# A two-layer convolution kernel: one program order for all engines in layer one, stores of a piece held back, borders written later

## The chip, the cores and the metric

The kernel runs on one core of a Trainium2 chip. The metric is the device time of one execution in microseconds, the median of several runs. A profiled execution of the same program gives the trace; it is one execution and has its own time.

## The reference, cut to what matters

The input x is 32 images of 8 channels, 256 x 256, float32. Layer zero runs on a group-normalised copy (4 groups of 2 channels each), layer one on the result of layer zero.

```python
def layer0(x):                      # x: group-normalised
    grid = x
    for _ in range(15):             # the lattice
        mapped = 3.9 * grid * (1 - grid)
        local = conv3x3(mapped, K_local, per channel)
        grid = 0.85 * (0.7 * mapped + 0.3 * local) + 0.15 * x
    cml = clip(grid, 1e-4, 1 - 1e-4)
    h = relu(conv3x3(x, Wp) + bp)                   # 8 -> 128 channels
    nca = sigmoid(conv1x1(h, Wu) + bu)              # 128 -> 8
    gin = concat([x, cml, nca])
    g = sigmoid(conv1x1(relu(conv3x3(gin, Wg1) + bg1), Wg2) + bg2)
    return g * cml + (1 - g) * nca

def layer1(x):                      # x: group-normalised
    sx, sw = 127 / max|x|, 127 / max|w|             # over the whole batch
    return conv3x3(round(x * sx), round(w * sw)) / (sx * sw) + bias

y = x + layer0(gn(x))
out = y + layer1(gn(y))
```

## The kernel before, in words

The program's "layer one" is its first big block (everything of `layer0` above); the second block, "layer two", does `layer1` and is not touched.

The images go in 8 groups of 4. For every group four kinds of work are needed, each written as a Python generator that emits some instructions and then yields a weight:

- **normalise** (L285 on, `prep`): for an image and a pair of channels ("piece"): load x (`xr`), statistics, mean and deviation over partitions by two tiny matmuls (L313, L324), scale in place (L331), then three copies: `xq` (ScalarE, L336, columns regrouped by four), `hi` (VectorE, L342, rounded) and `lo` (GpSimd, L343, the rest). Six DMAs store them to DRAM scratch (L345, L352). `xq`, `hi` and `lo` have one buffer each. A job is two pieces: channel pairs 0 and 1, or 2 and 3. A group has eight jobs.
- **lattice**: for each of the 8 channels, all four images of the group at once, 15 steps. A step is three tiles; a tile is 12 matmuls (L487) into two PSUM banks, and on VectorE two `gt` (L495) and two `m` (L500) operations; GpSimd mends an edge (L504). After tiles two and three SP issues the exchange of rows between neighbouring partitions (`m_a<-m_a`, L450 and L451). A channel of four images is a "unit"; its loads (`d_a`, `d_b`) and the stores of its result go into a list `later`, from which `background(3)` issues three DMAs after each tile (L444).
- **nca**: for each image, the hidden convolution (L567) in pairs of PSUM banks that ScalarE empties with relu (L577), then L584 down to 8 channels and a sigmoid. Rows are loaded to `im` (L537, L545).
- **gate**: for each image of the group before, ten pieces: loads `nb`, `cq`, `xb`; 54 matmuls in three parts (L759); r1 (L771); a small matmul (L725), sigmoid (L727); then GpSimd's `d` and `f` (L730, L732) and VectorE's product, sum, statistics, maximum and minimum (L734 to L745).

`together(lattice, filler)` emits a lattice step, then filler until both stand at the same share of their nominal weights; `both` mixes nca, gate and normalisation of the next group in the same way. So every lattice step on TensorE is followed by some filler on TensorE. Lattice tiles, the hidden convolution and the small matmuls share six PSUM banks (tag `pt`).

What sets the order: on TensorE the order in which the program emits (`manual_schedule` for PE). On VectorE, ScalarE, GpSimd and SP's DMA queue a planner puts the instructions in order before the run, by its own model of times and with the program's order as priority; on the chip each engine then runs its list in order. `reuse_waits` is not given for the pools of layer one.

Ahead of it all stands a preparation: constants, and zeros written to the border rows of 68 DRAM scratch tensors (4 DMAs each, ACT's queue, L199 and L202) from a tile `zt` in a pool that is freed before layer one's pools are opened. Normalisation of channel pairs 0 and 1 of the first four images is emitted before the lattice starts, pairs 2 and 3 as the first filler.

Of the kernel before, what the change touches and what calls it, by code (L numbers as in the profile page):

```python
# [31 lines left out]
F32 = mybir.dt.float32  # L32
# [8 lines left out]
P = 128  # L41
C = 8
# [71 lines left out]
def kernel(  # L114
# [46 lines left out]
    rstd_y = cp.tile([P, B], F32, name="rstd_y")  # L161
    dev_y = cp.tile([P, B], F32, name="dev_y")


# [7 lines left out]
    with tc.tile_pool(name="prep", bufs=1) as pp, tc.tile_pool(name="prep2", bufs=2) as pp2:  # L172
# [20 lines left out]

        zt = pp.tile([P, PW], F32, name="zt")
        G.memset(zt, 0.0)
        for t, n, w in (
            *((t, 2 * C, PW) for t in xp_s), *((t, C, W) for t in (*cm_s, *nc_s, *y_s))
        ):
            nc.scalar.dma_start(dram_ap(t, 0, [[w, n], [1, w]]), zt[:n, :w])  # L199
            for i in range(0, 11, 5):  # L200
                m = min(5, 11 - i) * n
                nc.scalar.dma_start(dram_ap(t, (257 + i) * n * w, [[w, m], [1, w]]), zt[:m, :w])  # L202

# [53 lines left out]
    with ExitStack() as one:  # L257

        one.enter_context(tc.manual_schedule(engines={mybir.EngineType.PE}))
        pool = lambda name, bufs, **kw: one.enter_context(tc.tile_pool(name=name, bufs=bufs, **kw))  # L260
        xp, sp2, gp, bp2, st = pool("xp", 4), pool("sp2", 1), pool("gp", 3), pool("bp2", 2), pool("st", 2)
        imp, hp, wk, wk1, np_ = pool("imp", 3), pool("hp", 12), pool("wk", 2), pool("wk1", 1), pool("np", 1)
        ps_c, ps_a = pool("ps_c", 6, space=PSUM), pool("ps_a", 2, space=PSUM)
# [24 lines left out]
        def normalise(jobs):  # L288

            def begin(b, half):
                xrs = []
                mv = st.tile([P, 2, 2], F32, name="mv", tag="mv")
                stats = st.tile([P, 2, 2, 6], F32, name="stats", tag="stats")
                for i in range(2):
                    g = 2 * half + i
                    xr = xp.tile([P, 2, 2, W], F32, name="xr", tag="xr")
                    nc.sync.dma_start(  # L300
                        xr.rearrange("p c h w -> p (c h) w"),
                        dram_ap(x, (b * C + 2 * g) * H * W, [[W, P], [P * W, 4], [1, W]]),
                    )
                    for j in range(2):
                        V.bn_stats(stats[:, i, j, :], xr[:, j].rearrange("p h w -> p (h w)"))
                    V.bn_aggr(mv[:, i, :], stats[:, i].rearrange("p j s -> p (j s)"))
                    xrs.append(xr)
                return b, half, xrs, mv

            def scale(b, half, xrs, mv):  # L310
                gs = slice(2 * half, 2 * half + 2)
                pm = ps_c.tile([P, 512], F32, name="pm", tag="pt")
                T.matmul(pm[:, 0:2], avg, mv[:, :, 0], start=True, stop=True)  # L313
                m, rstd = mean_x[:, b, gs], rstd_x[:, b, gs]
                V.tensor_copy(m, pm[:, 0:2])
                e = st.tile([P, 2], F32, name="e", tag="e")
                V.tensor_tensor(e, mv[:, :, 0], m, ALU.subtract)
                V.tensor_tensor(e, e, e, ALU.mult)
                V.tensor_tensor(e, e, mv[:, :, 1], ALU.add)
                return e  # L320

            def end(b, half, xrs, e):
                pv = ps_c.tile([P, 512], F32, name="pv", tag="pt")
                T.matmul(pv[:, 0:2], avg, e, start=True, stop=True)  # L324
                rstd = rstd_x[:, b, 2 * half : 2 * half + 2]
                V.tensor_scalar(rstd, pv[:, 0:2], GN_EPS, None, ALU.add)
                G.tensor_tensor(rstd, rstd, mhalf[:, 0:2], ALU.pow)
                for i, xr in enumerate(xrs):
                    g = 2 * half + i
                    flat = xr.rearrange("p c h w -> p (c h w)")  # L330
                    V.tensor_scalar(  # L331
                        flat, flat, mean_x[:, b, g : g + 1], rstd_x[:, b, g : g + 1],
                        ALU.subtract, ALU.mult,
                    )
                    xq = sp2.tile([P, 2, 2, 4, NJ], F32, name="xq", tag="xq")
                    S.activation(  # L336
                        xq.rearrange("p c h q j -> p (c h) q j"),
                        xr.rearrange("p c h (j q) -> p (c h) q j", q=4),
                        AF.Copy,
                    )  # L340
                    inner = lambda t: t[:, :, :, 1 : 1 + W]
                    V.tensor_copy(inner(hi), xr)  # L342
                    G.tensor_tensor(inner(lo), xr, inner(hi).bitcast(F32), ALU.subtract)  # L343
                    for h in range(2):
                        nc.sync.dma_start(  # L345
                            dram_ap(
                                xq_s[b % NBUF], (2 * g * H + P * h) * W, [[W, P], [H * W, 2], [1, W]]
                            ),
                            xq[:, :, h].rearrange("p c q j -> p c (q j)"),
                        )  # L350
                        for j, src in enumerate((hi, lo)):
                            nc.sync.dma_start(  # L352
                                dram_ap(
                                    xp_s[b % NBUF],
                                    (1 + P * h) * ROW + (C * j + 2 * g) * PW,
                                    [[ROW, P], [PW, 2], [1, PW]],
                                ),
                                src.bitcast(F32)[:, :, h, :],
                            )
                    yield 1.0  # L360
                ready.add((b, half))

            ahead = None
            for job in [*jobs, None]:
                now = begin(*job) if job else None
                yield 1.0
                if ahead:
                    e = scale(*ahead)
                    yield 1.0
                    yield from end(*ahead[:3], e)  # L370
                ahead = now

# [3 lines left out]
        def lattice(g):  # L376


            def load(u):


                c, out, dmas = u % C, [], []
                assert all((u // C * GB + i, c // 4) in ready for i in range(GB))
                for s in range(2):
# [57 lines left out]
            def background(n):  # L442
                for _ in range(min(n, len(later))):
                    nc.sync.dma_start(*later.pop(0))  # L444
                    issued[0] += 1

            def exchange(t, k):
# [109 lines left out]
        def nca(b):  # L557
# [80 lines left out]
            im = ahead  # L638
            if (b + 1, 0) in ready and (b + 1, 1) in ready:
                loaded[b + 1] = rows(b + 1, 0, 0)  # L640
# [26 lines left out]
        def stage(b, p, sc):  # L667
# [11 lines left out]
            )  # L679
            for k in range(n):  # L680
                G.tensor_copy(  # L681
                    cmb[:, k, 1 : 1 + W].rearrange("p (j q) -> p j q", q=4),
                    cq[:, k, :].rearrange("p (q j) -> p j q", q=4),
                )
            xb = bp2.tile([P, 2, W], F32, name="xb", tag="xb", bufs=3)
            if p in (0, 9):
                G.memset(xb, 0.0)
            for k in range(n):
# [6 lines left out]
                        [[W, r1_ - r0], [H * W, C], [1, W]],  # L695
                    ),
                )
            for k in range(n):
# [13 lines left out]
        def gate(b):  # L712
# [35 lines left out]
            last = done = None  # L748
            sc, ahead = staged.pop(b, None) or begin_gate(b)
            for p in range(10):  # L750
# [5 lines left out]
                for s, t in ((0, xnb), (1, cmb), (2, nb)):  # L756
# [11 lines left out]
                    if s < 2:  # L768
                        yield 2.6
                r1 = wk.tile([P, 512], F32, name="r1", tag="r1")  # L770
                S.activation(r1[:, : n * W], pa[:, : n * W], AF.Relu, bias=bv[:, 0:1])  # L771
# [93 lines left out]

        def prep(g, halves):
            return normalise([(b, half) for half in halves for b in range(g * GB, g * GB + GB)])

# [11 lines left out]
        T_NCA, T_GATE, T_PREP, T_LATTICE = 520.0, 340.0, 34.0, 8 * 45 * 1.97  # L880
        for _ in prep(0, (0,)):
            pass
        for g in range(NG):
            fill, t = images(nca, g), T_NCA
            if g:
                fill, t = both(fill, t, after(g - 1, images(gate, g - 1)), T_GATE), t + T_GATE
            if g + 1 < NG:
                fill, t = both(fill, t, prep(g + 1, (0, 1)), T_PREP), t + T_PREP
            if g == 0:
                fill, t = chain(prep(0, (1,)), fill), t + 20.0  # L890
            together(lattice(g), T_LATTICE, fill, t)
        for _ in images(gate, NG - 1):
            pass
# [115 lines left out]
```

## Time and profile before

| what | value |
|---|---|
| median of 3 runs | 14360.28 us (14354.44 to 14362.28) |
| profiled execution, time | 14416.5 us |
| its span, first to last instruction | 14414.7 us |
| mean granted TensorE clock | 0.963 |
| busy: TensorE matmul, VectorE, ScalarE, GpSimd | 92%, 57%, 28%, 17% of the span |
| first lattice matmuls | 201 us, in a steady row from 220 us |
| first matmul of the hidden convolution | 305 us, in a steady row from 316 us |
| layer two | from about 13640 us |

The span runs from the first to the last instruction. Busy shares are means over stages; a stage is read from its own stretch of time. A wait is written "engine line waiting <- engine line waited for"; "SPq" is SP's DMA queue. The granted clock of TensorE is either 1.0 or 0.5 at any time, and a matmul takes twice as long at 0.5.

### The profile page before, as it was taken

Reading aid. Unit: us, or ns where it says so; the run is one execution under the profiler, and the core shown is the slowest. Engines: PE = TensorE matmul, PEld = TensorE weight load, DVE = VectorE, ACT = ScalarE, POOL = GpSimd, SP = SyncE. Lnnn points to the kernel's source line nnn. Section 1 sums busy time; section 2 is a strip of 40 time slices with the busy share of each in tenths; the row PEclk is TensorE's granted clock in tenths of the full one; section 3 lists DMA queues with packets and bytes.
Section 4 is the critical chain, followed back from the end, with each engine's and each line's share of the span. In section 5 each row is a group of like instructions: output and inputs, shape, how many; then the busy total and the mean of one; then the engine's idle time right before and its main releaser. Section 6 shows DMA issues by size and latency. Waiting matters only on the chain.

```text
span 14414.7 us, 229163 instructions
## 1 busy us (share of the span) xinstructions
PE 13267.4 (92%) x81728; PEld 6423.3 (45%) x81728; DVE 8213.1 (57%) x16290; ACT 4039.8 (28%) x6274; POOL 2445.9 (17%) x4266
## 2 busy tenths in 40 slices
PE   2999999999999999999999999999999999999833
PEld 1554444444444444444444444444444444444311
DVE  3555555555555555555555555555555555555576
ACT  1333232232222222222322223222323222222122
POOL 1111111111111111111111111111111111112300
PEclk9999999999999999999999999999999999999966
DMA  5444444444444444444444434444444433333465
GB/s 148 93 97 92 90 103 106 103 94 100 110 94 100 99 106 94 103 100 95 100 103 107 98 93 106 110 94 94 104 104 98 103 88 88 80 83 78 122 195 176
DMA packets 2259559, 1496.74 MB, mean 104 GB/s; under 512 B 1061248, under 2 KB 2229504, under 8 KB 2258304
## 3 DMA queue, kind: packets, MB, share of 16 engines
q1 hardware_dynamic: 2176976, 1401.95, 41.9%
q10 hardware_dynamic: 81456, 80.12, 1.7%
q8 instruction: 664, 10.88, 0.3%
q14 instruction: 463, 3.79, 0.1%
HBM read 866.48 MB, written 478.69 MB: 93 GB/s over the span
## 4 chain that ended last, share of the span: by engine, by line
PE 70%; DMA 9%; DVE 9%; SPq 5%; issue 3%; POOL 2%; ACT 1%; ACTq 1%; POOLq 0%; DVEq 0%
PE pt L487 31%; PE ph L567 18%; PE pa L759 13%; PE acc L584 7%; DVE gt L495 2%; DMA im<-xp_s 1%; PE pg L725 1%; DMA xp_s<-lo 1%; SPq L545 1%; DVE m_b L500 1%; DMA xb<-in_x_dram 1%; DMA m_a<-m_a 1%; DMA out_dram<-ob 1%; SPq L960 1%; PE pt L953 1%
## 5 line engine op out<-in xcount | busy, mean ns | idle before, releaser
L487 PE MATMUL pt<-m_a,lw 128*64 128x390 f32 x17280 | 5827.0, 497 | 186.4 <-DMA m_a<-m_a 122.4
L487 PE MATMUL pt<-m_b,lw 128*64 128x384 f32 x17280 | 5796.6, 492 | 19.2 <-DVE m_b L410 18.0
L577 ACT ACTIVATE h<-ph,bp_sb 128x512 f32<-128x512 f32 x4096 | 2584.6, 684 | 6491.5 <-PE ph L567 6423.0
L487 PEld LDWEIGHTS pt<-m_a,lw 128*64 128x64 f32 x17280 | 2298.4, 138 | 1884.0 <-issue 1681.2
L487 PEld LDWEIGHTS pt<-m_b,lw 128*64 128x64 f32 x17280 | 2306.6, 138 | 1560.0 <-issue 1423.6
L567 PE MATMUL ph<-im,wp_hi 48*128 48x512 f32 x12288 | 2800.2, 419 | 174.2 <-DVE gt L495 113.1
L567 PE MATMUL ph<-im,wp_lo 48*128 48x512 f32 x12288 | 2675.2, 402 | 0.0
L495 DVE SCALAR_TENSOR_TENSOR gt<-pt,d_b 128x390 f32<-128x390 f32 x2880 | 1605.3, 557 | 1714.7 <-PE pt L487 1711.2
L495 DVE SCALAR_TENSOR_TENSOR gt<-pt,d_a 128x384 f32<-128x384 f32 x2880 | 1580.3, 549 | 1694.5 <-PE pt L487 1694.1
L504 POOL TENSOR_TENSOR m_b<-m_b,junk 128x12 f32<-128x12 f32 x2688 | 795.5, 296 | 8193.8 <-DVE m_b L500 7517.2
L567 PEld LDWEIGHTS ph<-im,wp_hi 48*128 48x128 f32 x12288 | 1417.5, 189 | 1081.7 <-DVE gt L495 303.9
L500 DVE SCALAR_TENSOR_TENSOR m_b<-gt 128x390 f32<-128x390 f32 x2688 | 1546.1, 575 | 44.5 <-DVE gt L495 2.3
L500 DVE SCALAR_TENSOR_TENSOR m_a<-gt 128x384 f32<-128x384 f32 x2688 | 1522.3, 566 | 17.2
L567 PEld LDWEIGHTS ph<-im,wp_lo 48*128 48x128 f32 x12288 | 1417.0, 189 | 217.3
L584 PE MATMUL acc<-h,wu_z 128*32 128x512 f32 x8320 | 1165.6, 603 | 6.1 <-ACT nca L602 5.5
L759 PE MATMUL pa<-xnb,gw 128*64 128x512 f32 (+1 forms) x3840 | 879.9, 588 | 43.7 <-DVE xnb L700 43.5
L759 PE MATMUL pa<-cmb,gw 128*64 128x512 f32 (+1 forms) x3840 | 857.6, 577 | 17.4 <-POOL cmb L681 17.4
L759 PE MATMUL pa<-nb,gw 128*64 128x512 f32 (+1 forms) x3840 | 863.6, 576 | 0.0
L730 POOL TENSOR_TENSOR d<-cmb,nb 128x512 f32<-128x512 f32 x320 | 502.9, 1572 | 1460.6 <-DVE gate L734 1028.5
L700 DVE TENSOR_SCALAR xnb<-xb,sc 128x256 f32<-128x256 f32 x608 | 290.7, 493 | 796.7 <-DMA xb<-in_x_dram 759.5
L953 PE MATMUL pt<-qt,qw 128*128 128x512 bf16 (+1 forms) x960 | 269.5, 451 | 477.0 <-ACT ob L954 425.4
L734 DVE TENSOR_TENSOR gate<-gate,d 128x512 f32<-128x512 f32 x320 | 217.4, 679 | 764.7 <-ACT gate L727 756.7
(132 smaller groups left out, 6928.0 us busy)
## 6 DMA issues: line engine op xcount, KB each, us to landing
im<-xp_s SPq DMA_DIRECT2D x1152, 193.5 KB
im<-xp_s SPq DMA_DIRECT2D x1216, 96.8 KB
d_a<-xq_s SPq DMA_DIRECT2D x2048, 36.0 KB
nb<-nc_s SPq DMA_DIRECT2D x288, 256.0 KB
cq<-cm_s SPq DMA_DIRECT2D x288, 256.0 KB
yb<-y_s ACTq DMA_DIRECT2D x29, 2432.0 KB
xb<-in_x_dram SPq DMA_DIRECT2D x544, 128.0 KB
xp_s<-hi SPq DMA_DIRECT2D x256, 258.0 KB
```

The costliest lines, as they stand in the source:

```text
L487: T.matmul(pt[half], lw[:, c, k, half], beside if part == 2 else own, start=part < 2, stop=part > 0,)
L495: V.scalar_tensor_tensor(gt, pt, FLOOR, d[:, ts, :], ALU.max, ALU.add)
L500: V.scalar_tensor_tensor(to, gt, 1.0, gt, ALU.subtract, ALU.mult)
L504: G.tensor_tensor(edge, edge, junk.unsqueeze(1).to_broadcast([P, 6, 2]), ALU.mult)
L567: T.matmul(ph[:, :n].rearrange("p (h w) -> p h w", w=W), w[64 * i : 64 * i + 48, dx, :], rhs[:, :, dx : dx + W], start=(dx == 0 and w is w ...
L577: S.activation(h[:, :n], ph[:, :n], AF.Relu, bias=bp_sb)
L584: T.matmul(acc[32 * g : 32 * g + 32, :cols], wu_z[:, 24 - 8 * i : 56 - 8 * i], h, start=first, stop=last,)
L700: V.tensor_scalar(xnb[:, k, 1 : 1 + W], xb[:, k, :], sc[:, i : i + 1], sc[:, 1:2], ALU.subtract, ALU.mult,)
L730: G.tensor_tensor(three(d), cmb[:, :n, 1 : 1 + W], nin, ALU.subtract)
L734: V.tensor_tensor(y[:, :cols], gt[:, :cols], d[:, :cols], ALU.mult)
L759: T.matmul(three[half], gw[:, s * 3 + dx, half], t[:, :n, dx : dx + W], start=(i == 0), stop=(i == 8),)
L953: T.matmul(pt, qw[:, dx, :], q[:, k0 : k0 + n, dx : dx + W], start=(dx == 0), stop=(dx == 2))
```

## The change

1. All engines and SP's queue keep the order in which the program emits in layer one (`manual_schedule()` without a list of engines), and the pools wait tile by tile for memory that others have used.
2. The zeros lie in a constant tile of 64 columns. Each border DMA reads it several times over (256-byte or 172-byte pieces). Sixteen border DMAs, those of the first four `xp_s`, stay in front; 256 are issued from SP's queue by `background` during the first group, in the places that `later` leaves.
3. Normalisation: loads are split from statistics (`take`), which come after the work on the job before. The six stores of a piece are not issued after it but just before the next piece is scaled (`pending`).
4. First group: pair 0 of the four images before the lattice, then pair 1, then jobs of pairs 2 and 3, as the first filler.
5. Gate: the loads of a piece are split from what VectorE and GpSimd do with them (`arrange`), which is emitted two thirds of a piece later; the first piece of a group gets two units of other work between them.

```diff
+    zt = cp.tile([P, 64], F32, name="zt")
...
+            k = 64 if w == W else 43
+            for row, m in ((0, 1), (257, 5), (262, 5), (267, 1)):
+                borders.append(
+                    (
+                        dram_ap(t, row * n * w, [[w, m * n], [k, w // k], [1, k]]),
+                        zt[: m * n, :k].unsqueeze(1).to_broadcast([m * n, w // k, k]),
+                    )
+                )
+        for _ in range(4 * GB):
+            nc.scalar.dma_start(*borders.pop(0))
...
-        one.enter_context(tc.manual_schedule(engines={mybir.EngineType.PE}))
-        pool = lambda name, bufs, **kw: one.enter_context(tc.tile_pool(name=name, bufs=bufs, **kw))
...
+        one.enter_context(tc.manual_schedule())
+
+        pool = lambda name, bufs, **kw: one.enter_context(
+            tc.tile_pool(name=name, bufs=bufs, reuse_waits="tile", **kw)
+        )
+        hp, xp, sp2, gp, bp2 = pool("hp", 12), pool("xp", 4), pool("sp2", 1), pool("gp", 3), pool("bp2", 2)
...
+            def stores(b, g, xq):
+                for h in range(2):
+                    nc.sync.dma_start(
+                        dram_ap(xq_s[b % NBUF], (2 * g * H + P * h) * W, [[W, P], [H * W, 2], [1, W]]),
+                        xq[:, :, h].rearrange("p c q j -> p c (q j)"),
+                    )
+                for h in range(2):
+                    for j, src in enumerate((hi, lo)):
+                        nc.sync.dma_start(
+                            dram_ap(
+                                xp_s[b % NBUF],
+                                (1 + P * h) * ROW + (C * j + 2 * g) * PW,
+                                [[ROW, P], [PW, 2], [1, PW]],
+                            ),
+                            src.bitcast(F32)[:, :, h, :],
+                        )
+                ready.add((b, g))
+
+            pending = []
...
+                for g, xr in zip(gs, xrs):
+                    if pending:
+                        stores(*pending.pop())
                     flat = xr.rearrange("p c h w -> p (c h w)")
                     V.tensor_scalar(
                         flat, flat, mean_x[:, b, g : g + 1], rstd_x[:, b, g : g + 1],
...
                     inner = lambda t: t[:, :, :, 1 : 1 + W]
                     V.tensor_copy(inner(hi), xr)
                     G.tensor_tensor(inner(lo), xr, inner(hi).bitcast(F32), ALU.subtract)
...
+                    pending.append((b, g, xq))
                     yield 1.0
...
             for job in [*jobs, None]:
                 now = begin(*job) if job else None
-                yield 1.0
+                yield 0.5
                 if ahead:
                     e = scale(*ahead)
                     yield 1.0
                     yield from end(*ahead[:3], e)
-                ahead = now
+                ahead = take(*now) if job else None
+                yield 0.5
+            stores(*pending.pop())
...
             def background(n):
                 for _ in range(min(n, len(later))):
                     nc.sync.dma_start(*later.pop(0))
+                    n -= 1
                     issued[0] += 1
+                if g == 0 and units.keys() - {0}:
+                    for _ in range(min(n, len(borders))):
+                        nc.sync.dma_start(*borders.pop(0))
...
+                if p < 9:
+                    ahead = arrange(*ahead)
+                elif b + 1 in staged:
+                    staged[b + 1] = staged[b + 1][0], arrange(*staged[b + 1][1])
...
-        for _ in prep(0, (0,)):
+        for _ in prep(0, ((0,),)):
             pass
...
-                fill, t = chain(prep(0, (1,)), fill), t + 20.0
+                fill, t = chain(prep(0, ((1,), (2, 3))), fill), t + 30.0
             together(lattice(g), T_LATTICE, fill, t)
+            while borders:
+                nc.sync.dma_start(*borders.pop(0))
```

## The prediction

> **What bounds the kernel now.** I read the page's shares and its row of 40 slices first, then a table of stretches, then the waits, and last the timeline around one normalisation piece.
>
> ```profile
> PE 13267.4 (92%) x81728; PEld 6423.3 (45%) x81728; DVE 8213.1 (57%) x16290; ACT 4039.8 (28%) x6274; POOL 2445.9 (17%) x4266
> ...
> PE   2999999999999999999999999999999999999833
> ...
> PEclk9999999999999999999999999999999999999966
> ```
>
> TensorE is the bound: 92% of the span, nine tenths in every slice but the first and the last three (layer two, which the change leaves alone). The stretches give the sizes (busy time of PE, PEld, DVE, ACT, POOL, then the clock and the DMA share):
>
> ```profile
> 0.00:220.00 220.00, 6.05 (x18) 4.22 (x18) 49.13 (x149) 20.20 (x15) 22.88 (x54) 1.00 0.49 139
> 220.00:320.00 100.00, 42.26 (x177) 21.09 (x179) 56.52 (x129) 20.44 (x16) 24.89 (x24) 0.66 0.69 191
> 320.00:1840.00 1520.00, 1435.15 (x9263) 748.50 (x9261) 843.38 (x1732) 468.15 (x731) 161.33 (x397) 0.96 0.43 94
> 1840.00:11400.00 9560.00, 9324.60 (x58070) 4537.00 (x58072) 5500.38 (x11473) 2750.11 (x4285) 1754.56 (x3030) 0.98 0.44 101
> ```
>
> TensorE does nothing to speak of for 220 us and is full from about 320 us. From 350 to 13250 us the trace has 316 us of idle TensorE and 370 us of busy TensorE at half clock. With half of the latter as loss, that is 316 + 185 = 501 us: everything that a better order could win in the long middle. Who waits for whom (total us, times, longest):
>
> ```profile
> ACT xq L336 <- DMA xq_s<-xq: 240.7, 46, 8.1
> ...
> DVE hi L342 <- DMA xp_s<-hi: 195.2, 51, 9.5
> ...
> PE pt L487 <- DMA m_a<-m_a: 122.4, 74, 6.5
> PE ph L567 <- DVE gt L495: 113.1, 151, 4.0
> ...
> SPq L300 <- DMA y_s<-zt: 92.5, 5, 91.3
> ```
>
> The last line is the head: SP holds the first load of x for 91 us until the border DMAs have landed, because the load's buffer lies where the zeros lay. The first two lines matter most for what follows: the normalisation (L331 to L352) has one buffer each for xq, hi and lo, so each piece waits until the stores of the piece before have landed. The timeline shows what one such wait does:
>
> ```profile
> 4666.08 1.71 SPq L345 DMA_DIRECT2D xq_s<-xq  x1
> ...
> 4667.85 0.46 SPq L352 DMA_DIRECT2D xp_s<-hi  x1
> ...
> 4672.14 2.04 ACT L336 ACTIVATE xq<-xr 128x1024 f32<-128x1024 f32 x1 [4.08 <-DMA xq_s<-xq]
> 4672.90 0.69 DVE L342 CAST hi<-xr 128x1024 fp32r<-128x1024 f32 x1 [2.60 <-DMA xp_s<-hi]
> ...
> 4674.07 0.69 ACT L727 ACTIVATE gate<-pg,bv 128x512 f32<-128x512 f32 x1
> ...
> 4674.81 0.79 PE L567 MATMUL ph<-im,wp_hi 48*128 48x512 f32 x1 [3.18 <-ACT gate L727]
> ```
>
> ScalarE stands 4.08 us before xq; the sigmoid behind it comes late, the PSUM bank that it frees comes late, and TensorE idles 3.18 us. The granted clock then falls to half for 6.83 us: some 6.6 us for one wait.
>
> **What the skill says.** The Trainium skill's "TensorE: Matmul & The Clock Gate", Part 1 on the HAM clock gate: a window of about 3.4 us without enough work halves the clock until a busy window has passed. The trace agrees: half-clock periods of 3.41 and 6.83 us follow even gaps of 1.4 to 3 us. Its "DMA: Bandwidth & Descriptors", section on the anatomy of one DMA: a semaphore wait happens on the issuing sequencer, so what stands behind a waiting DMA in SP's queue waits too; and it gives about 2 us fixed per DMA. The trace has more: from the end of the issue of a hi store to the cast that waited for it 4.6 us at 4673 and 6.1 us at 5369. Its "Perfetto Trace Analysis", Optimization Strategy: a gap that repeats can mean too few buffers. Here xq, hi and lo are that case.
>
> **The change, part by part.** *Head.* The border wait goes: of 272 border issues 16 stay in front, and the first load of x moves from 113.9 us to where SP is done with the weights, 15.6 us. VectorE builds constants until 32.4 us, so the first statistics come at about 33 instead of 117.9. Four pieces (one channel pair of four images) replace eight before the lattice. Pieces follow each other at 9 us (hi casts at 153, 163, 172, 181, 189 us): the fourth hi cast at about 66, its last store issued at 73. Before, the last store was issued at 194.8 and lattice matmuls ran steadily from 220, 25 us later, behind 36 loads. So the lattice starts at about 98 us, 122 earlier. But twelve pieces instead of eight must now pass before layer zero's hidden convolution (L567) has work, and in program order they alternate with lattice steps: 28.5 units of work at 4.9 a step are 6 steps. 12 x 9 us plus 6 x 9 us for the vector part of a step is 162, plus 12 for the last stores and row loads: work from 98 + 162 + 12 = 272 us, against 316. With one or two lattice steps more done by then (6 to 7 against 5, some 6 us each) the head gives 44 + 6 = **-50 us**, between 0 and -110.
>
> *Borders in SP's queue.* 256 issues at 0.35 us in group zero are 90 us of SP over 1400 us, at most three per tile, behind the exchange of that tile. Their packets are 172 and 256 bytes, but 35 thousand of 2.26 million. SP is about half busy (some 15 issues of 0.5 us per step of 13.5 us). Nothing, with +15 us if that cover is gone.
>
> *Normalisation in the steady state.* This is the step that decides. The stores of a piece are no longer issued after it but just before the next piece writes the same buffers. In program order the pieces lie 50 us or more apart (four units a job, eight jobs a group of about 1670 us), so an immediate store would long have landed; now every piece meets stores that have only just been issued. I took all 732 whole lattice steps between 2000 and 13000 us from the timeline; the medians from the start of a step: TensorE done at 6.1 us, first vector operation at 2.2, last m at 8.5, last exchange issued at 10.1, next step at 13.5. SP can't pass that exchange before 10.1. With up to 2.8 us of other loads before it (5.6 issues per step) it starts the six stores at 10.1 to 13; the second xq store is issued 1 us later, the last hi store 2.5 us later; landing takes 5 to 6 us. So xq is free at about 17 to 20 and hi at 18 to 21. VectorE comes to hi at about 9.5, waits 8 to 11 us, and reaches the next step's first gt (wanted at 13.5 + 2.2 = 15.7) 3 to 6 us late. Behind ScalarE's waiting xq (2.1 us itself) stand the relus of this filler, which free the PSUM banks that the next step's second tile needs at 15.5: they come at 20 or later, 5 us late. Where the piece comes after the filler's matmuls only VectorE's delay counts, and the slack between gt and the next use of its bank (2.7 us) leaves 1 to 3 us. Mean idle 3.5 us, half clock after most of them 1.7 to 3.4 more: 5 us a piece is my value. There are 7 x 16 = 112 steady pieces: 560 us. What they cost now: in the stretches from 5 us before to 14 us after each hi cast, 12.9% of the middle, lie 177 us of the 501; less the share of the rest, 48, that is 129 us for 56 pairs, of which the second of each pair waits. Net **+430 us**. Bounds: each wait costs what a pair costs now, 2.3 us, gives 258 - 129 = +130; 7 us as in the shown example gives 784 - 129 = +655. Below nothing would need a piece cheaper than 1.15 us; with a wait of 8 us against a slack of 7 I find no reason for that, but a SP that arrives early would do it.
>
> *Order of the rest.* 372 us of the 501 lie outside those stretches. Exchanges come right behind their vector operation, the gate's loads a piece ahead (DVE waits for xb and POOL for cq fall away, both hidden now); the 5.7 us stop at each group's first gate piece is filled by two units, 6 x (5.7 + 3). Against it, VectorE waits in order for sigmoid and d before 3.6 us of gate work, as it nearly does now. I take -60, from -185 (half) to +100.
>
> *Last group's gate and layer two.* 390 and 775 us, same instructions: 0.
>
> Sum on the profiled execution's span: 14414.7 - 50 + 430 - 60 = 14735 us. The profiled execution took 14416.5 where the median of the runs is 14360.3, 56 less: **14680 us**, 2.2% slower.
>
> **Rivals.** *The stores land in cover* (0.25, faster): SP reaches the stores early, or TensorE's filler bridges the wait, and a piece costs 1 us. Then -50 - 60 + 112 - 129 = -127: 14235 us. It decides from below 2.1 us a piece (112 x 2.1 = 129 + 110). For it: first pieces of a pair wait for nothing now; against: the exchange holds SP until 10.1 us. *Order hardly matters* (0.05): the order written out by the scheduler was already nearly the program's, piece losses at 2.3 us just take the gains: 14360 +/- 29. *ScalarE and VectorE in order become the bound* (0.10): pieces and gate pieces meet in one filler (every third), POOL's d and f queue behind the waiting lo, and 10 us a piece are lost: 1120 - 129 - 110 = +880, 15240 us.
>
> **How the numbers follow.** The likeliest case has 0.60 and its own range is 14440 (+130 - 50, middle unchanged) to 14905 (+655 - 50 - 60). To leave out no more than 2 in 10 the range goes down into the faster case, to 14210, and up to 14950. 0.2% is about what a measurement of this kernel can tell from no change. Faster 0.25, same 0.05, slower 0.60 + 0.10 = 0.70.
>
> **What would show it.** Right: first load of x near 16 us, lattice from about 98 us, L567 from about 272; waits of xq L336 and hi L342 for their stores over 112 times with 5 us or more each, 600 to 900 us in all; half-clock periods at each piece; a step's mean in groups one to six about 0.5 us longer. Wrong: these waits at 3 us or less with TensorE's share above 93%, or exchange waits (m_a) that grow, which would mean SP's queue is the cause.

## The result, and the profile after

The changed kernel takes 15394.29 us (median; 15375.36 to 15403.19) where the kernel before takes 14357.36: ratio 1.072, 95% interval 1.0702 to 1.0739. It is 1037 us slower; forecast were 14680 us, some 320 us slower, in a range up to 14950.

The page after, shares and rows of slices:

```profile
span 15373.6 us, 226505 instructions
...
PE 13644.4 (89%) x81744; PEld 6559.6 (43%) x81744; DVE 8922.7 (58%) x16310; ACT 4018.2 (26%) x6274; POOL 2127.4 (14%) x4270
...
PE   4888899999999999999999999999999999999833
...
PEclk7999999999999999999999999999999999999966
```

TensorE's share falls from 92% to 89%, and its busy time grows by 377 us although the matmuls are the same: more of them run at half clock (from 350 to 13250 us, 994 us of busy time at half clock instead of 370; in the trace before, the lattice matmuls that read m_a start 328 ns apart at full clock and 651 ns apart at half, in the median). The stretches after (same columns as before) show a better head and a worse middle:

```profile
0.00:220.00 220.00, 54.72 (x220) 27.05 (x220) 98.65 (x260) 29.01 (x24) 35.36 (x77) 0.81 0.51 132
220.00:320.00 100.00, 42.07 (x222) 23.03 (x224) 35.73 (x70) 17.75 (x17) 14.65 (x16) 0.64 0.53 139
320.00:1840.00 1520.00, 1335.18 (x8314) 708.38 (x8312) 811.11 (x1553) 425.83 (x671) 111.92 (x345) 0.93 0.42 89
1840.00:11400.00 9560.00, 8893.33 (x53692) 4269.79 (x53686) 5556.51 (x10593) 2520.05 (x3950) 1400.42 (x2802) 0.95 0.40 93
```

Between 1840 and 11400 us TensorE does 53692 matmuls instead of 58070. What comes after the last lattice matmul, the last group's gate and layer two, kept its length (1170 us instead of 1164). Counted as for the prediction (idle time plus half of the busy time at half clock), the loss up to 350 us is 245 us instead of 286, and the loss from 350 us to the last lattice matmul 1432 instead of 501. The waits:

```profile
ACT xq L374 <- DMA xq_s<-xq: 1388.2, 114, 22.6
DVE hi L380 <- DMA xp_s<-hi: 1157.3, 118, 14.4
...
POOL lo L381 <- DMA xp_s<-lo: 517.3, 45, 15.9
...
PE ph L595 <- DVE gt L523: 372.0, 289, 7.1
...
PE pt L515 <- ACT h L605: 106.5, 31, 9.7
...
PE pt L515 <- DMA m_a<-m_a: 92.5, 76, 5.1
```

Nearly every piece now stands before its own predecessor's stores, 12 us for xq and 10 us for hi in the mean, while the waits for the exchange (m_a) are shorter in total than before. One piece in the timeline:

```profile
5944.08 0.81 DVE L369 TENSOR_SCALAR xr<-xr,mean_x,rstd_x 128x1024 f32<-128x1024 f32 x1 [1.00 <-POOL rstd_x L364]
...
5945.62 0.94 SPq L340 DMA_DIRECT2D xq_s<-xq  x2
...
5947.70 0.70 SPq L346 DMA_DIRECT2D xp_s<-hi  x1
...
5952.71 0.69 DVE L380 CAST hi<-xr 128x1024 fp32r<-128x1024 f32 x1 [7.82 <-DMA xp_s<-hi]
5953.32 2.60 DVE L731 TENSOR_SCALAR xnb<-xb,sc 128x256 f32<-128x256 f32 x2
...
5956.19 0.52 DVE L523 SCALAR_TENSOR_TENSOR gt<-pt,d_b 128x390 f32<-128x390 f32 x1
...
5956.77 0.79 PE L595 MATMUL ph<-im,wp_hi 48*128 48x512 f32 x1 [4.88 <-DVE gt L523]
```

SP issues the last hi store at 5947.70; the cast waits 7.82 us for its landing; behind it stand two gate scalings (1.3 us each, while GpSimd works on lo) and the last two of the statistics, and only then the lattice's gt, whose matmuls began at 5946. TensorE has no free bank and idles 4.88 us.

### The profile page after: what moved, and what is told of

Same layout as the page of the kernel before. It is cut to its first block, busy times and chain, and to the rows that moved or that the text cites. A ratio compares the mean times of both kernels' runs of the same rounds, so it can differ in the third digit from the quotient of the medians.

```text
span 15373.6 us, 226505 instructions
## 1 busy us (share of the span) xinstructions
PE 13644.4 (89%) x81744; PEld 6559.6 (43%) x81744; DVE 8922.7 (58%) x16310; ACT 4018.2 (26%) x6274; POOL 2127.4 (14%) x4270
## 4 chain that ended last, share of the span: by engine, by line
PE 60%; DVE 14%; DMA 10%; SPq 10%; issue 4%; POOL 1%; ACT 1%; DVEq 0%; POOLq 0%; ACTq 0%
PE pt L515 24%; PE ph L595 16%; PE pa L794 12%; PE acc L612 6%; DVE gt L523 5%; DVE m_a L528 3%; DMA xp_s<-hi 2%; SPq L468 2%; DMA im<-xp_s 2%; SPq L573 1%; SPq L478 1%; SPq L479 1%; PE pg L756 1%; DMA d_a<-xq_s 1%; DMA out_dram<-ob 1%
## 5 line engine op out<-in xcount | busy, mean ns | idle before, releaser
L515 PE MATMUL pt<-m_a,lw 128*64 128x390 f32 x17280 | 5830.1, 499 | 155.0 <-DMA m_a<-m_a 92.5
L595 PE MATMUL ph<-im,wp_hi 48*128 48x512 f32 x12288 | 2944.8, 431 | 503.0 <-DVE gt L523 372.0
L595 PE MATMUL ph<-im,wp_lo 48*128 48x512 f32 x12288 | 2801.5, 415 | 0.0
L595 PEld LDWEIGHTS ph<-im,wp_hi 48*128 48x128 f32 x12288 | 1497.8, 196 | 1478.2 <-DVE gt L523 836.6
L532 POOL TENSOR_TENSOR m_b<-m_b,junk 128x12 f32<-128x12 f32 x2688 | 580.7, 216 | 10364.6 <-DVE m_b L528 9734.6
L528 DVE SCALAR_TENSOR_TENSOR m_a<-gt 128x384 f32<-128x384 f32 x2688 | 1615.2, 601 | 92.6
L595 PEld LDWEIGHTS ph<-im,wp_lo 48*128 48x128 f32 x12288 | 1499.3, 197 | 239.1
L612 PE MATMUL acc<-h,wu_z 128*32 128x512 f32 x8320 | 1207.0, 622 | 72.6 <-ACT h L605 72.6
L380 DVE CAST hi<-xr 128x1024 fp32r<-128x1024 f32 x128 | 88.8, 694 | 1171.5 <-DMA xp_s<-hi 1157.3
L765 DVE TENSOR_TENSOR gate<-gate,d 128x512 f32<-128x512 f32 x320 | 344.3, 1076 | 698.5 <-ACT gate L758 495.6
L810 ACT ACTIVATE r<-pa,bv 128x512 f32<-128x512 f32 x320 | 212.7, 665 | 1727.4 <-PE pa L794 1727.2
```

Source lines behind the costliest of these rows:

```text
L515: T.matmul(pt[half], lw[:, c, k, half], beside if part == 2 else own, start=part < 2, stop=part > 0,)
L528: V.scalar_tensor_tensor(to, gt, 1.0, gt, ALU.subtract, ALU.mult)
L532: G.tensor_tensor(edge, edge, junk.unsqueeze(1).to_broadcast([P, 6, 2]), ALU.mult)
L595: T.matmul(ph[:, :n].rearrange("p (h w) -> p h w", w=W), w[64 * i : 64 * i + 48, dx, :], rhs[:, :, dx : dx + W], start=(dx == 0 and w is w ...
L612: T.matmul(acc[32 * g : 32 * g + 32, :cols], wu_z[:, 24 - 8 * i : 56 - 8 * i], h, start=first, stop=last,)
L765: V.tensor_tensor(y[:, :cols], gt[:, :cols], d[:, :cols], ALU.mult)
```

## The experiments

Each changes the changed kernel, but for e3, which changes the kernel before. "Before" is measured on the same chip as the run. e1 to e4, e5 to e8 and e9 to e12 ran on three chips, so between these groups the ratios are compared. A difference of ratios is given in points: one point is a hundredth of the kernel before, 144 us.

| run | edit | median us | ratio to before (95%) |
|---|---|---|---|
| e1 | stores right after their piece | 14543.53 | 1.0133 (1.0118 to 1.0148) |
| e2 | stores half a unit after it | 14638.47 | 1.0200 (1.0185 to 1.0215) |
| e3 | kernel before, program order alone | 16381.13 | 1.1412 (1.1395 to 1.1429) |
| e4 | changed kernel, planner's order | 14145.47 | 0.9859 (0.9842 to 0.9875) |
| e5 | e1, d and f earlier | 14435.76 | 1.0045 (1.0028 to 1.0062) |
| e6 | only xq stores held back | 14600.92 | 1.0156 (1.0141 to 1.0171) |
| e7 | only hi and lo stores held back | 15209.70 | 1.0575 (1.0559 to 1.0591) |
| e8 | e1, planner's order | 14197.26 | 0.9872 (0.9858 to 0.9887) |
| e9 | e1, gate loads joined to their users | 15948.88 | 1.1108 (1.1092 to 1.1125) |
| e10 | e4, d and f earlier | 14159.96 | 0.9864 (0.9847 to 0.9880) |
| e11 | e4, gate loads joined to their users | 14285.19 | 0.9951 (0.9937 to 0.9966) |
| e12 | only hi stores held back | 15053.59 | 1.0488 (1.0472 to 1.0503) |

**Are the held-back stores the cause, or the order?**

e1:

```diff
-                    if pending:
-                        stores(*pending.pop())
...
-                    pending.append((b, g, xq))
+                    stores(b, g, xq)
...
-            stores(*pending.pop())
```

> The six stores of a piece are issued right after the piece, as in the kernel before; all else as in the changed kernel. Theory A (the held-back stores, issued just before the next piece overwrites xq, hi and lo, cost most of the gain lost): in the changed kernel the stretches from 16 us before to 14 us after a hi cast hold 874 us of loss beyond the usual, and most of it goes: 14600 to 14800 us; the waits of ScalarE's xq and VectorE's hi for their stores fall from 1388 and 1157 us to under 400 us together. Theory B (it is the program's order of the normalisation chain as such, with statistics, tiny matmuls and the power on GpSimd in line): 15200 us or more. Theory C (SP, now waiting for the copies, holds back the exchanges): the waits fall but those of TensorE for m_a grow past 300 us, 15000 or more.

e2:

```diff
-                    if pending:
-                        stores(*pending.pop())
...
                     pending.append((b, g, xq))
-                    yield 1.0
+                    yield 0.5
+                    stores(*pending.pop())
+                    yield 0.5
...
-            stores(*pending.pop())
```

> The stores of a piece are issued half a unit of filler after it and half a unit before the next piece, so that neither SP waits for the copies nor the copies for the stores. Theory A: as e1 or better, 14550 to 14750 us, waits of xq and hi for their stores under 200 us together in the steady state. Theory B: 15200 us or more. Theory C: clearly better than e1, by 100 us or more.

e3:

```diff
-        one.enter_context(tc.manual_schedule(engines={mybir.EngineType.PE}))
+        one.enter_context(tc.manual_schedule())
```

> The kernel before with one edit: all engines and SP's queue keep the program's order in layer one. Stores stay right after their piece, gate loads and their users stay together, the border zeros stay in front. Theory A (order alone costs what the changed kernel loses outside the normalisation, about 170 us, and has no gain at the head): 14450 to 14700 us. Theory D (program order itself is the main cost, whatever the stores do): 15100 us or more.

e4:

```diff
-        one.enter_context(tc.manual_schedule())
+        one.enter_context(tc.manual_schedule(engines={mybir.EngineType.PE}))
```

> The changed kernel with the planner's order again on VectorE, ScalarE, GpSimd and SP (only TensorE keeps the program's order). The planner is free to issue the held-back stores as soon as they are ready. Theory A: the waits for stores go back to what they were before and the head's 41 us stay: 14250 to 14400 us. Theory E (what costs is the new emission on TensorE, with borders, single-pair jobs and split gate loads): 14900 us or more.

e1 gives back 851 of the 1037 us, a little more than theory A said; theories B and C fall. Its waits, whole run:

```profile
PE ph L592 <- DVE gt L520: 85.0, 167, 2.0
...
DVE hi L378 <- DMA xp_s<-hi: 33.1, 9, 7.6
...
ACT xq L372 <- DMA xq_s<-xq: 9.2, 2, 6.2
```

So under program order the place of six DMA issues is worth 5.5% of the changed kernel. In e2 neither side waits for long (44 us for hi), yet it is 95 us slower than e1: within theory A's range, but not "as e1 or better". No harm from SP's waiting for the copies shows: the waits of TensorE for m_a are 160 us in e1 and 186 in e2. Why half a unit later is worse was not followed up.

e3 was a miss for theory A, and theory D holds for that kernel: the order alone costs 2024 us. Its waits point to a reason, which e9 tests:

```profile
DVE xnb L700 <- DMA xb<-in_x_dram: 2556.9, 358, 20.3
POOL cmb L681 <- DMA cq<-cm_s: 2522.9, 310, 19.0
...
PE ph L567 <- DVE gt L495: 942.4, 662, 13.8
```

Loads and what uses them are emitted together there; in program order VectorE then stands before a load that has just been issued, with the lattice behind it. It is the same pattern as with the stores, on the other side of the buffer.

e4 beats the kernel before by 1.4%, and by more than theory A said (14250 us at best). Its waits for stores are back at about the size of before:

```profile
DVE hi L380 <- DMA xp_s<-hi: 271.3, 61, 11.2
...
ACT xq L374 <- DMA xq_s<-xq: 160.8, 40, 11.4
```

Theory E falls: what costs is not the new emission but the order in which VectorE, ScalarE, GpSimd and SP run it.

**Which of the three waits counts?** e6, e7 and e12 hold back a part of the stores. For e6 and e7 `stores` is split in two; e12 does the same with hi alone:

```diff
-            def stores(b, g, xq):
+            def store_xq(b, g, xq):
...
+            def store_hilo(b, g, xq):
...
                     if pending:
-                        stores(*pending.pop())
+                        store_xq(*pending.pop())      # e7: store_hilo
...
+                    store_hilo(b, g, xq)              # e7: store_xq
                     pending.append((b, g, xq))
```

> The changed kernel, with only the two stores of xq held back; hi and lo are stored right after the piece. So only ScalarE meets fresh stores. Theory A1 (ScalarE's relus free the PSUM banks, so its wait carries the larger part of the 851 us between e1 and the changed kernel): 15000 to 15250 us. Theory A2 (VectorE's wait carries it): 14550 to 14850 us.

> The changed kernel, with only the four stores of hi and lo held back; xq is stored right after the piece. So VectorE and GpSimd meet fresh stores and ScalarE does not. Theory A1: 14700 to 14950 us. Theory A2 (the waits of TensorE for gt are 372 us in the changed kernel and 85 in e1, those for relus 213 and 28, so VectorE's share is some six tenths): 15050 to 15350 us.

> The changed kernel, with only the two stores of hi held back; xq and lo are stored right after the piece. Theory A3 (VectorE alone, standing before hi, carries what e7 showed): 15000 to 15250 us. Theory A4 (GpSimd before lo, with the edges of the lattice queued behind it, carries half or more): 14600 to 14900 us.

Theory A2 holds clearly, A1 falls: over e1, xq alone adds 0.23 points (33 us, with intervals that overlap), hi and lo 4.42 (635 us), hi alone 3.55 (510 us). In e6 ScalarE waits nearly as long as in the changed kernel. TensorE's waits for gt stay as in e1, and those for relus rise to 134 us from 28, but those for the exchange fall to 102 from 160:

```profile
ACT xq L376 <- DMA xq_s<-xq: 1260.2, 101, 23.1
...
PE pt L519 <- DMA m_a<-m_a: 101.7, 81, 5.0
...
PE ph L599 <- DVE gt L527: 81.5, 174, 2.0
...
PE acc L616 <- ACT h L609: 73.8, 7, 12.2
```

In e7 it is the other way round, 364 us of waits for gt:

```profile
DVE hi L382 <- DMA xp_s<-hi: 962.6, 114, 13.3
...
POOL lo L383 <- DMA xp_s<-lo: 544.0, 51, 15.3
...
PE ph L599 <- DVE gt L527: 364.1, 348, 6.4
```

e12:

```profile
POOL lo L391 <- DVE hi L390: 978.1, 123, 21.0
...
DVE hi L390 <- DMA xp_s<-hi: 795.2, 118, 11.6
...
PE ph L606 <- DVE gt L534: 267.1, 291, 4.2
...
PE pt L526 <- DMA m_a<-m_a: 182.0, 104, 8.8
```

So the hi stores alone bring most of it. GpSimd stands in e12 too, because lo reads hi. But late edges would show as waits for the exchange, and these are 182 us against 160 in e1, while waits for gt are 267 against 85: the loss comes mainly through VectorE.

xq and hi/lo together (5.87 points over e1) cost more than the sum of the two alone (4.65). In the traces the surplus lies at the relus. TensorE waits for them 213 us in the changed kernel and 27 us in e7, while its waits for gt do not grow (461 and 493 us, all lines). So ScalarE's wait, which costs little alone, adds 1.45 points (208 us) on top of the others. That the xq stores stand ahead of the hi stores in SP's queue can be a part of it (the mean wait of hi is 9.8 us, in e7 8.4); it was not tried apart.

Two buffers each for xq, hi and lo, the direct remedy for a wait of this kind, were not tried.

**What is left between e1 and the kernel before?** e5 moves GpSimd's part of a gate piece:

```diff
+                    if s == 0 and last:
+                        df = blend(*last)     # d and f, on GpSimd
                     if s < 2:
                         yield 2.6
...
-                    done = finish(*last)
+                    done = finish(*last, df)
```

> e1 (stores right after their piece, program order on all engines) with one move: GpSimd's d and f of a gate piece are emitted two thirds of a piece earlier, so that they neither stand beside VectorE's gate work nor are waited for. Theory F (part of the 186 us that e1 is still above the kernel before comes from GpSimd and VectorE meeting on the same gate piece: the product takes 1.08 us on average instead of 0.68, and VectorE waits 140 us for d): product back to about 0.7 us, wait for d under 30 us, 14400 to 14480 us. Theory G (VectorE has room enough; what is left is the order of the loop itself): 14520 us or more.

The groups of VectorE's product, first e1, then e5 (busy, mean ns, idle before and its releasers):

```profile
L762 DVE TENSOR_TENSOR gate<-gate,d 128x512 f32<-128x512 f32 x320 | 347.7, 1087 | 664.3 <-ACT gate L755 474.0 <-POOL d L758 139.8 <-issue 30.1
```

```profile
L768 DVE TENSOR_TENSOR gate<-gate,d 128x512 f32<-128x512 f32 x320 | 222.9, 696 | 628.1 <-ACT gate L765 574.6 <-issue 53.4
```

Theory F holds: the product is back to 0.70 us, no wait for d is left, and the ratio falls by 0.88 points, some 126 us. The Trainium skill's "SBUF — State Buffer", section on the two separate sides, says that a GpSimd operation that reads SBUF and a VectorE operation with two SBUF inputs take a shared pair of ports in turn, the one that comes second blocking for the whole instruction of the other. The traces agree. In e1, 155 of the 320 products run while GpSimd's f runs, each time with f begun first, some 0.11 us before; the product then takes 1.66 us in the median and ends 0.55 us after f, and without f it takes 0.69 (the profile's spans of GpSimd are rough). In e5 six products overlap an f, in the kernel before 13. VectorE's 608 scalings to xnb became shorter as well, 0.54 us instead of 0.71 in the mean. How much of the 126 us is the meeting, how much these scalings and how much the wait for d is open, since e5 changed all three. e5 is still 0.45% above the kernel before.

e9 joins the gate's loads to their users again, under program order:

```diff
+            for k in range(n):
+                G.tensor_copy(
...
-            return xnb, xb, cmb, nb, cq, k0, n, sc
-
-        def arrange(xnb, xb, cmb, nb, cq, k0, n, sc):
...
-            if b not in staged:
-                staged[b] = begin_gate(b)
-                yield 2.0
-                staged[b] = staged[b][0], arrange(*staged[b][1])
-            sc, ahead = staged.pop(b)
+            sc, ahead = staged.pop(b, None) or begin_gate(b)
...
-                if p < 9:
-                    ahead = arrange(*ahead)
...
```

> e1 (program order on all engines, stores right after their piece, head of the change) with the gate's loads joined again to the copies and scalings that use them, as in the kernel before. Theory I (joined loads under program order are what made the order alone cost 2024 us: VectorE and GpSimd stand 2557 and 2523 us before the loads of a gate piece): 15900 to 16400 us, with waits of xnb for xb and of cmb for cq over 2000 us each. Theory J (the old head and other parts made most of it): under 15300 us.

```profile
DVE xnb L725 <- DMA xb<-in_x_dram: 2621.6, 362, 20.0
POOL cmb L706 <- DMA cq<-cm_s: 2609.9, 316, 19.2
```

Theory I holds: 1405 us over e1, nearly 10%. So the change's split of loads from users was necessary for its own order of engines; the same thought was not applied to the stores.

**What does the planner need of it?** e8, e10 and e11 put the planner's order under e1, under d and f earlier, and under joined loads.

> e4 (planner's order on all engines but TensorE, rest of the change kept) with the stores right after their piece. Theory A (the planner issues held-back stores early anyway): 14145 us within 60. Theory H (the planner profits from the late place of the stores, because SP is freed for exchanges): 14250 us or more.

> e4 (the change with the planner's order on all engines but TensorE) and d and f two thirds of a piece earlier. Theory K (the planner places d and f well anyway): within 30 us of e4's 14145. Theory F in full (it helps there too): 14000 to 14100 us.

> e4 with the gate's loads joined again to their users: what is left of the change is the head, the borders, the order of the first group, the pools and the held-back stores, all under the planner. Theory L (the head gives the part of e4's 212 us that lies before 350 us, 83, and the split of the gate's loads most of the other): 14220 to 14300 us. Theory M (the planner moves loads ahead by itself, so the split is worth nothing): 14120 to 14180 us.

e8 and e4 differ by 0.13 points, with intervals that overlap: under the planner no effect of the place of the stores shows (theory A). e10 equals e4 (theory K). e11 stands between: the head and what goes with it give 0.5 points, the split loads another 0.9 (theory L; M falls). VectorE's wait for xb hardly changes by the split (656 us in e11, 631 in e4), but TensorE's wait for xnb falls from 53 to 9 us and that for gt from 96 to 50. So e4 is the best version found, 212 us under the kernel before. Waiting for memory tile by tile, the part of the change on the pools, is in all of these runs but e3 and was not tried alone.

## Why the prediction was wrong, by its steps

**Direction and main mechanism: right.** The step "normalisation in the steady state" named the stores that have only just been issued, the single buffers and VectorE's late return to the lattice, and said that this decides. e1, e7 and e12 show it. The waits for stores come with the frequency that was named (114 and 118 times, over 112), and over the whole run the signs of being wrong did not come: TensorE's share fell, and the exchange waits did not grow.

**Its size: wrong, and this is the failed step.** Forecast were 560 us for the pieces, +430 after what they cost before (129), at most +655. By the trace, the stretches from 16 us before to 14 us after a hi cast hold 874 us beyond the usual, 7.8 us a piece instead of 5 (bound 7), so +745. The 851 us between the changed kernel and e1, whose pieces hold some 30 us by the same count, agree with the 874. Two terms were mis-sized. First, VectorE's lateness: I had 3 to 6 us. The first gt after a hi cast, against its usual 2.2 us after the step's first matmul, comes 7.8 us late in the median piece and a little under 6 us in the mean (kernel before about 2, e1 under 1). I had let the lattice follow the cast at once and left out other filler between them, as the 2.60 us of xnb above; and I took a median step, where the step in the example was followed by the next after 11.5 us and not 13.5. Second, the split of the blame: for pieces early in a step I priced ScalarE's blocked relus at 5 us, and VectorE's delay alone at no more than 1 to 3 us. It was the other way round: VectorE's and GpSimd's waits alone cost 635 us (e7), ScalarE's alone 33 (e6), and 208 on top of the others. The hi wait itself was forecast well: 8 to 11 us, measured 9.8 in the mean. It rested on measured landings. The figure of about 2 us that the prediction sets beside them, from the Trainium skill's "DMA: Bandwidth & Descriptors", section on the anatomy of one DMA, is another quantity: it is given for DMAs that GpSimd issues and leaves out the time of the data, while the 4.6 and 6.1 us are whole landings from SP's queue. The forecast of 600 to 900 us in all for xq and hi was far off (2546 us), because I summed no more than 5 to 8 us per piece there, against my own 8 to 11 us for hi alone.

**Order of the rest: wrong sign.** Forecast -60, worst +100. The loss outside the pieces in the middle grew from 372 (501 - 129) to 558 us (1432 - 874), +186. e1 agrees: it is 186 us above the kernel before although its head loses 218 us instead of 286, so the order costs about 250 us behind the head. Some 126 of them go with the place of GpSimd's d and f (e5). The prediction has no term for the two engines slowing each other and says that VectorE waits for sigmoid and d "as it nearly does now"; in the planner's order they seldom met (product 0.68 us, in the changed kernel 1.08). Where the other half lies stays open. That the gate's loads fall away as waits was right (xb from 759.5 to 35.9 us, cq from 619.9 to 156.2).

**Head: close.** Forecast -50; the loss up to 350 us fell by 41. The first lattice matmuls come at 77 us and steadily from about 97 (forecast 98), L595 at 287 instead of 272. Without the held-back stores L592 starts at 250 us: the same wait cost the head too, which I had left out by pricing twelve pieces at the pace of immediate stores. (The hi casts from the fifth to the fourteenth take 118 to 252 us in the changed kernel and 116 to 214 in e1.)

**Borders in SP's queue: little harm, if any.** Over the whole run the waits of TensorE for the exchange fell (122.4 to 92.5 us). From 320 to 1840 us, where the borders are issued, they rose from 46.5 to 59.2 us (e4 60.4), which would fit the 15 us that the prediction gave for lost cover. e4 and e11, which have the borders there too, are faster than the kernel before. They were not tried alone.

**From the profiled execution to the median.** I took 56 us off because the profiled execution of the kernel before was that much above its median. The changed kernel's own span, 15373.6 us, lies 21 below its median: the offset belonged to one execution and not to the program. Together, from the forecast 320 us to the measured 1037: the pieces +315 (745 against 430), the rest of the order +246 (186 against -60), the head +9, this offset +77, and 69 us by which the span grew beyond the losses counted here. The pieces alone take the sum above the range.

**The rivals.** That the stores land in cover fell with e1, that order hardly matters with e3. The third, VectorE and ScalarE as the bound with 10 us a piece at 15240 us, came nearest. Its mechanism, GpSimd's d and f behind a waiting lo, is not the larger part by e12: hi alone costs 510 of the 635 us of hi and lo, mainly through gt.

## What to carry to other kernels

With engines in program order, put a buffer's store a full landing before the next write into it, and a load a full landing before its first use, counted in the emitted order and including what the issuing queue itself waits for. Here breaking this cost 5.9 points for the stores (e1) and 9.8 for the gate's loads (e9), through the work queued behind. The planner hid such mistakes, the stores' wholly as far as can be told (e8), the loads' down to 0.9 points (e11): take it away only with all of them mended, or keep it and take the other gains alone (e4). When a wait on one engine is priced, count everything that stands between it and the critical instruction, not the wait against the mean slack.

## What the runs showed that was not expected

- Six DMA issues per piece, moved from just before the next piece to right after their own, are worth 851 us (5.5%) under program order and nothing that shows (0.13 points) under the planner.
- ScalarE can stand 1260 us before its stores at a cost of 33 us, while 960 us of VectorE and 540 of GpSimd cost 635 (both against e1). Together they cost 851.
- Half of VectorE's gate products took 1.66 us instead of 0.69 where program order lets them begin just behind GpSimd's f.
- Program order alone, with nothing else changed, cost 14%, twice the loss of the whole change (7.2%).
